# State tiles of four states by 32 channels in a decoder layer with a state-space block, in place of two by 64

## The chip, the cores and the metric

The kernel runs on one core of a Trainium2 chip. The time is the device time of one execution in microseconds (us); for the kernel before it is 5500.68 us, the median of three runs (5499.43 to 5505.06). Five engines take part: TensorE (PE) multiplies matrices and loads weights (PEld), VectorE (DVE) and ScalarE (ACT) work element by element, GpSimd (POOL) does a few small things and indirect transfers, and SyncE (SP) has the queue from which nearly all transfers (DMAs) are issued.

## What is computed

The reference is one decoder layer on x of 8 sequences x 512 tokens x 512 features, all in float32: a state-space (Mamba) block, cross-attention with 16 heads, and a mixture of 32 experts with a shared expert, each followed by a layer norm. The change is in the state-space block. Cut to that part (1024 channels d, 16 states n per channel):

```python
dA  = jnp.exp(A[None, None] * dt[..., None])                     # A = -exp(A_log), [d, n]
dBx = dt[..., None] * B_ssm[:, :, None, :] * x_main[..., None]

def scan_fn(h, inp):
    dA_t, dBx_t, C_t = inp
    h = dA_t * h + dBx_t                                         # [batch, d, n]
    y_t = jnp.einsum('bdn,bn->bd', h, C_t)                       # sum over the 16 states
    return (h, y_t)

y = ys + x_main * D_param
y = y * jax.nn.silu(z)
out = res_scale * (y @ out_proj_w) + residual
```

So each of the 16384 pairs (channel, state) has its own recurrence over 512 tokens; B and C depend on the state and the token but not on the channel, dt and x on the channel and the token but not on the state.

## The kernel before

**Tiles and steps.** Tokens go through the state-space block in chunks of T = 256, two to a sequence, 16 in all. Within a chunk, channels come in pairs of 128-channel tiles (index q, four pairs; i or ci says which of the two), and states in four groups (g). A step treats 128 channels x 4 states x 256 tokens, so a chunk has 32 steps and the kernel 512. The 128 partitions of a step's tile hold 64 channels twice, once for each half of the four states; along a row lie four blocks of 256 tokens, for two halves of channels (j) by two states (m).

A step does this:

- `decays` (L473): four exponentials on ACT, 128x256 each, write dA into one of two tiles `da`; dt comes from `both` (below).
- `carry` (L479): ACT copies the last state of the previous chunk into the first column of each block of a new tile `h` (four buffers).
- `steps_in` (L486): DVE multiplies dt*x by B into `h` (128x1024).
- `scan` (L493): DVE runs the recurrence along the whole row, 128x1028.
- `keep` (L498): ACT saves the last column for the next chunk.
- `collect` (L503): DVE multiplies `h` by C in place; then `products` has PE sum over the states. A product with the constant `twice` (128x64, two identity matrices of 64 one above the other) adds the two halves of the partitions; four such products of 256 columns add into `py` in PSUM, 64 partitions each. At g = 0 a product with the identity brings in D*x first.
- `gated` (L536), once per pair of channel tiles: DVE multiplies `py` by silu(z).

**Copies to other partitions.** B and C are computed for a chunk by `x_proj` and spilled to DRAM (`scr`). `bcast` (L411) reads two states of each back into every partition of a half, once for each q and g: four DMAs of 128 KB, six buffers. dt and dt*x are computed for a pair of channel tiles by `prepare` (L424) at step 3 of eight; its part `both` copies them into tiles whose halves of the partitions hold the same channels: eight DMAs of 128 KB, two buffers each.

**What lies beside the steps.** Between the DVE operations of the steps (`run(0)`, `run(1)`, `run(2)`) stand the other parts of the layer: projections for this chunk and the next (`convolve`, `gate_x`), the output product of the last chunk (`back`), and, in small pieces taken from a list by weight, the cross-attention, router and shared expert of the previous sequence (`units`). Of these the trace's views name: the convolution's taps (L376, `xs`), the softplus for dt (L445, L449, `dtx`), silu of z (L393), `dense`, the products of 512 columns at full width of the projections (L755), and in the attention the copies of a head's query and key rows (L804 to L808, `l_qa`, `l_ka`), the products for the scores (L818, L844), their maximum over keys on DVE (L820, `mx`), its copy into the query's rows (L834, `nm`) and the weighted sum of values (L860). `products` of a step are called in the next step, behind that step's scan. The framework then orders the instructions on each engine by its own estimate of when each is ready, so an engine's order isn't exactly that of the program. Each engine and SP's queue work strictly in the order they were given. After the 512 steps come the attention of the last sequence and the experts; the change doesn't touch them.

## Time and profile before

| | |
|---|---|
| median of three runs | 5500.68 us |
| the profiled execution: its time | 5514.39 us |
| its span, first to last instruction | 5512.7 us |
| PE busy | 4898.5 us (89%) |
| DVE busy | 4267.8 us (77%) |
| ACT busy | 2566.4 us (47%) |
| DMA packets | 769.84 MB, mean 140 GB/s |
| mean granted TensorE clock | 0.939 |
| steps of the state-space block | 64 to 3655 us |
| B and C to all partitions (L418) | 1024 DMAs of 128 KB |
| dt and dt*x to both halves (L458) | 512 DMAs of 128 KB |
| sums over states (L526) | 4096 records (two a product), 638.0 us busy |

A line of the groups reads: source line, engine, operation, written tile <- read tiles, shape, count | busy time in us, mean ns of one | idle time of the engine just before them, and what ended most of it. A line of waits reads: engine, tile and line that waited <- what ended the wait: us in total, times, longest. PEclk is the share of its full clock that TensorE was granted. Busy time is an average over stages with different limits, so stretches of the span are read one by one.

### The profile page before, as it was taken

To read this page: it belongs to the slowest core of one execution; us is meant where nothing else is said; L and a number is where in the kernel's file an instruction comes from. 1 tells how busy PE (TensorE), PEld (TensorE's weight loads), DVE (VectorE), ACT (ScalarE), POOL (GpSimd) and SP (SyncE) were. 2 spreads that over 40 slices of the span, in tenths; PEclk is the share of its full clock that TensorE was granted. 3 is DMA by queue.
4 is the path that set the end of the run, shared out by engine and by line. 5 is a ranking of instruction groups with operands and counts; after the bars stand their busy time and mean duration, and the time that the engine had idled before them with its cause. 6 is when DMAs were issued, how large, how long until landed. Compare 5 with 4: busy or idle time off the path is not lost. (4 is left out here: it accounts for less than half of the span.)

```text
span 5512.7 us, 60257 instructions
## 1 busy us (share of the span) xinstructions
PE 4898.5 (89%) x19752; PEld 2733.6 (50%) x19752; DVE 4267.8 (77%) x5370; ACT 2566.4 (47%) x5696; POOL 508.9 (9%) x424
## 2 busy tenths in 40 slices
PE   6668889899988988988998898889899999999994
PEld 3334344334434434443443443333577777777773
DVE  7898989889889898998989989953455665655554
ACT  5455555565556555556555655523222222222223
POOL 1000001001000100100100010010111111111111
PEclk8778999999999999999999999989999999999997
DMA  6887356345534635634553463441344454445454
GB/s 183 236 236 210 105 145 187 110 120 176 149 108 115 214 85 140 189 114 115 167 161 105 116 209 91 128 149 37 122 120 121 118 127 126 124 122 126 115 123 145
DMA packets 554283, 769.84 MB, mean 140 GB/s; under 512 B 135810, under 2 KB 268450, under 8 KB 551921
## 3 DMA queue, kind: packets, MB, share of 16 engines
q1 hardware_dynamic: 517952, 677.55, 42.0%
q0 software_dynamic: 33280, 76.90, 7.4%
q10 hardware_dynamic: 2736, 11.54, 0.5%
q8 instruction: 157, 2.57, 0.2%
q14 instruction: 158, 1.29, 0.1%
HBM read 508.68 MB, written 165.05 MB: 122 GB/s over the span
## 5 line engine op out<-in xcount | busy, mean ns | idle before, releaser
L496 DVE TENSOR_TENSOR_SCAN h<-l_da,h 128x1028 f32<-128x1028 f32 x512 | 1170.2, 2292 | 23.6 <-ACT h L483 5.6
L477 ACT ACTIVATE l_da<-both,l_aneg 128x256 f32<-128x256 f32 x2048 | 890.7, 499 | 362.4 <-DVE h L496 324.5
L526 PE MATMUL py<-h,l_twice 128*64 128x256 f32 x4096 | 638.0, 417 | 159.3 <-DVE h L506 111.7
L489 DVE TENSOR_TENSOR h<-both,bc 128x1024 f32<-128x1024 f32 x512 | 619.3, 1215 | 149.9 <-PE py L526 74.4
L506 DVE TENSOR_TENSOR h<-h,bc 128x1024 f32<-128x1024 f32 x512 | 621.2, 1218 | 6.1
L526 PEld LDWEIGHTS py<-h,l_twice 128*64 128x64 f32 x4096 | 304.5, 146 | 493.7 <-issue 232.8
L818 PE MATMUL ps_s<-l_ka,l_qa 64*128 64x512 f32 x1024 | 345.3, 698 | 155.0 <-DVE mx L820 153.8
L1307 PE MATMUL ps_h<-xT,w 128*128 128x320 f32 x1536 | 435.8, 433 | 0.0
L1387 POOL DMA_INDIRECT based<-y,xe x160 | 251.9, 1575 | 1316.4 <-ACT y L1410 571.9
L820 DVE TENSOR_REDUCE mx<-ps_s 128x2 f32<-128x1024 f32 x256 | 310.5, 1216 | 77.7 <-PE ps_s L818 76.5
L1328 DVE TENSOR_TENSOR hT<-ps_h,p 128x320 f32<-128x320 f32 x128 | 62.9, 492 | 379.2 <-PE ps_h L1307 379.2
L1307 PEld LDWEIGHTS ps_h<-xT,w 128*128 128x128 f32 x1536 | 292.5, 191 | 118.3 <-issue 0.5
L860 PE MATMUL po<-eT,l_va 128*64 128x512 f32 x1024 | 292.9, 647 | 11.2 <-ACT eT L848 7.5
L844 PE MATMUL ps_t<-l_qa,l_ka 64*128 64x512 f32 x1024 | 292.7, 642 | 8.6 <-ACT eT L848 8.5
L848 ACT ACTIVATE eT<-ps_t 128x1024 f32<-128x1024 f32 x256 | 259.2, 1013 | 67.4 <-PE ps_t L844 67.1
L501 ACT COPY l_state<-h 128x4 f32<-128x4 f32 x256 | 49.9, 195 | 511.6 <-DVE h L496 511.5
L1307 PE MATMUL ps_h<-t,s 128*128 128x320 f32 x1024 | 286.1, 432 | 0.0
L342 PE MATMUL ps_x<-xnT,wm 128*128 128x256 f32 x1024 | 252.8, 403 | 1.2 <-ACT xnT L331 1.0
L818 PEld LDWEIGHTS ps_s<-l_ka,l_qa 64*128 64x128 f32 x1024 | 94.3, 199 | 314.8 <-DVE mx L820 241.8
L342 PE MATMUL ps_z<-xnT,wm 128*128 128x256 f32 x1024 | 246.3, 395 | 4.3 <-DVE o L566 2.7
L755 PE MATMUL ps_p<-x2T,wa 128*128 128x512 f32 x512 | 247.8, 635 | 0.9 <-DVE hT L947 0.7
L693 POOL DMA_INDIRECT xbuf<-x2t,dest x128 | 183.4, 1433 | 625.1 <-DVE dest L684 281.8
(229 smaller groups left out, 7603.3 us busy)
## 6 DMA issues: line engine op xcount, KB each, us to landing
bc<-scr SPq DMA_DIRECT2D x1024, 128.0 KB
w<-in_w SPq DMA_DIRECT2D x93, 1024.0 KB
wm<-in_in_proj_w SPq DMA_DIRECT2D x128, 512.0 KB
xbuf<-zero SPq DMA_DIRECT2D x32, 1362.5 KB
xe<-xbuf SPq DMA_DIRECT2D x32, 1362.5 KB
both<-dt SPq DMA_DIRECT2D x256, 128.0 KB
both<-dtx SPq DMA_DIRECT2D x256, 128.0 KB
wm<-in_out_proj_w SPq DMA_DIRECT2D x64, 512.0 KB
```

Source lines behind the costliest of these rows:

```text
L342: nc.tensor.matmul(ps[:, i, :], w[:, dc, i * P : (i + 1) * P], f["xnT"][:, dc, :], start=(dc == 0), stop=(dc == DC - 1),)
L477: nc.scalar.activation(da[:, n, 1:], dt[:, c % 2, j, :], AF.Exp, scale=aneg[:, c, j, g, m : m + 1])
L489: nc.vector.tensor_tensor(steps, dtx[:, c % 2].unsqueeze(2).to_broadcast([P, 2, NG // 2, T]), bc[0], ALU.mult)
L496: nc.vector.tensor_tensor_scan(flat, da.rearrange("p n t -> p (n t)"), flat, 0.0, ALU.mult, ALU.add)
L506: nc.vector.tensor_tensor(steps[:, :, :, 0:T], steps[:, :, :, 1:], bc[1], ALU.mult)
L526: nc.tensor.matmul(py[j * HP : (j + 1) * HP, c % 2, :], twice, h[:, j * 2 + m, 0:T], start=False, stop=(s == (NST // NG - 1, NG // 2 - 1, 1)),
L818: nc.tensor.matmul(ps[:, j, :], qa[r, lt * P : (lt + 1) * P], ka[r, :], start=True, stop=True)
L820: return lambda: nc.vector.tensor_reduce(mx[:, lt, :].unsqueeze(2), ps, AX.X, ALU.max) and None
L844: nc.tensor.matmul(ps[:, j, :], ka[r, kc * P : (kc + 1) * P], qa[r, :], start=True, stop=True)
L848: nc.scalar.activation(eT, ps, AF.Exp)
L860: nc.tensor.matmul(po[j * 2 * HD : (j + 1) * 2 * HD, :], va[:, kc, i, j * HD : (j + 2) * HD], eT[:, j, :], start=(kc == 0), stop=(kc == SC ...
L1307: nc.tensor.matmul(ps, w[:, n, r * P : (r + 1) * P], x[:, n, :], start=not more and n == 0, stop=n == 1, skip_group_check=more,)
```

## The change

A step's tile now holds four quarters of the partitions: 32 channels, once for each of four groups of four states (`NQ = 4`, `QP = 32`). Along a row lie four blocks of 256 tokens, for two of the four groups of 32 channels (j) by the two channel tiles of the pair (i). A step is now (q, g, jj): state g of each group of four, and half jj of the channels of both tiles. There are still 32 steps in a chunk, of the same size.

- Two steps (jj = 0, 1) are summed together: `collect` keeps the first tile in `f["half"]`, and `products` of the second issues four products with `fold` (128x32, four identity matrices of 32) of 512 columns each, into 32 partitions of `py` each. The identity product is one of 128 partitions x 512 columns.
- B and C of a chunk are fetched once (`bcast`, for one g: eight DMAs of 32 KB) and kept for all four q, in eight buffers.
- dt and dt*x are copied by `repeat` into one tile for each of dt/dt*x and jj, one buffer each, in eight DMAs of 64 KB. The copy for the next pair is called for dt*x right after the last `steps_in` that reads the old one, for dt after the exponentials of steps 6 and 7 of eight.

```diff
@@ -27,8 +27,10 @@
 NT_ = T // P
-NG = 4
-HP = P // 2
+NG = NST // 4
+NQ = 4
+QP = P // NQ
+NB = 4
 NPB = 3
@@ -111,7 +113,7 @@
     mp = ctx.enter_context(tc.tile_pool(name="l_mamba", bufs=1))
-    bcp = ctx.enter_context(tc.tile_pool(name="l_bc", bufs=6))
+    bcp = ctx.enter_context(tc.tile_pool(name="l_bc", bufs=2 * NST // NG))
     cp = ctx.enter_context(tc.tile_pool(name="l_const", bufs=1))
@@ -127,8 +129,10 @@
 
-    twice = cp.tile([P, HP], F32, name="l_twice")
-    nc.vector.tensor_tensor(twice, ident[:, 0:HP], ident[:, HP:P], ALU.add)
+    fold = cp.tile([P, QP], F32, name="l_fold")
+    nc.vector.tensor_tensor(fold, ident[:, 0:QP], ident[:, QP : 2 * QP], ALU.add)
+    for r in range(2, NQ):
+        nc.vector.tensor_tensor(fold, fold, ident[:, r * QP : (r + 1) * QP], ALU.add)
 
@@ -187,14 +191,14 @@
 
-    aneg = cp.tile([P, CC, 2, NST // NG, NG // 2], F32, name="l_aneg")
+    aneg = cp.tile([P, CC, NQ, NG], F32, name="l_aneg")
 
 
     conv_tail = cp.tile([P, CC, 3], F32, name="l_conv_tail")
-    state = cp.tile([P, CC, NST // NG, NG], F32, name="l_state")
-    nothing = cp.tile([P, NG, 1], F32, name="l_nothing")
+    state = cp.tile([P, CC // 2, NG, 2, NB], F32, name="l_state")
+    nothing = cp.tile([P, NB, 1], F32, name="l_nothing")
     nc.gpsimd.memset(nothing, 0.0)
-    das = [mp.tile([P, NG, T + 1], F32, name=f"l_da{i}") for i in range(2)]
+    das = [mp.tile([P, NB, T + 1], F32, name=f"l_da{i}") for i in range(2)]
     for da in das:
...
@@ -411,15 +413,24 @@
         got = []
-        for r0 in (g * NG, NST + g * NG):
-            t = bcp.tile([P, NG // 2, T], F32, tag="bc", name="bc")
-            for r in range(2):
-                n0 = r0 + r * NG // 2
+        for r0 in (g, NST + g):
+            t = bcp.tile([P, T], F32, tag="bc", name="bc")
+            for s in range(NQ):
                 nc.sync.dma_start(
-                    t[r * HP : (r + 1) * HP], f["scr"][n0 : n0 + NG // 2, :].partition_broadcast(HP)
+                    t[s * QP : (s + 1) * QP], f["scr"][r0 + s * NG, :].partition_broadcast(QP)
                 )
-            got.append(t.unsqueeze(1).to_broadcast([P, 2, NG // 2, T]))
-        return got
+            got.append(t.unsqueeze(1).to_broadcast([P, NB, T]))
+        f["bc", g] = got
+
+    def repeat(f, q, what, jj):
+
+        to = mp.tile([P, 2, 2, T], F32, tag=f"rep{what}{jj}", name="rep")
+        src = f["ready", q][what]
+        for s in range(NQ):
+            for j in range(2):
+                r0 = (2 * jj + j) * QP
+                nc.sync.dma_start(to[s * QP : (s + 1) * QP, j], src[r0 : r0 + QP])
+        f["rep", what, q, jj] = to
 
@@ -450,13 +461,7 @@
                 nc.vector.tensor_tensor(dtx, dt, f["xs"][q], ALU.mult)
-                f["ready", q] = []
-                for src in (dt, dtx):
-                    to = mp.tile([P, 2, 2, T], F32, tag=f"both{len(f['ready', q])}", name="both", bufs=2)
-                    for r in range(2):
-                        for j in range(2):
-                            nc.sync.dma_start(to[r * HP : (r + 1) * HP, :, j, :], src[j * HP : (j + 1) * HP])
-                    f["ready", q].append(to)
+                f["ready", q] = dt, dtx
                 return wait(timesD)
@@ -470,66 +475,59 @@
 
-    def decays(c, g, dt, da):
-
-        for n in range(NG):
-            j, m = n // 2, n % 2
-            nc.scalar.activation(da[:, n, 1:], dt[:, c % 2, j, :], AF.Exp, scale=aneg[:, c, j, g, m : m + 1])
-
-    def carry(t, c, g):
-
-        last = state[:, c, g].unsqueeze(2)
-        h = mp.tile([P, NG, T + 1], F32, tag="h", name="h", bufs=4)
+    def decays(f, q, g, jj, da):
+
+        dt = f["rep", 0, q, jj]
+        for n in range(NB):
+            j, i = n // 2, n % 2
+            nc.scalar.activation(
+                da[:, n, 1:], dt[:, j, i, :], AF.Exp, scale=aneg[:, 2 * q + i, 2 * jj + j, g : g + 1]
+            )
+
+    def carry(t, q, g, jj):
+
+        last = state[:, q, g, jj].unsqueeze(2)
+        h = mp.tile([P, NB, T + 1], F32, tag="h", name="h", bufs=4)
         nc.scalar.copy(h[:, :, 0:1], last if t else nothing)
         return h
 
-    def steps_in(c, h, dtx, bc):
-
-        steps = h.rearrange("p (j m) t -> p j m t", j=2)[:, :, :, 1:]
+    def steps_in(f, q, g, jj, h):
+
+        dtx = f.pop(("rep", 1, q, jj)) if g == NG - 1 else f["rep", 1, q, jj]
         nc.vector.tensor_tensor(
-            steps, dtx[:, c % 2].unsqueeze(2).to_broadcast([P, 2, NG // 2, T]), bc[0], ALU.mult
+            h[:, :, 1:], dtx.rearrange("p j i t -> p (j i) t"), f["bc", g][0], ALU.mult
         )
 
-    def scan(t, c, g, da, h):
+    def scan(da, h):
 
         flat = h.rearrange("p n t -> p (n t)")
         nc.vector.tensor_tensor_scan(flat, da.rearrange("p n t -> p (n t)"), flat, 0.0, ALU.mult, ALU.add)
 
-    def keep(t, c, g, h):
+    def keep(t, q, g, jj, h):
 
         if t < S // T - 1:
-            nc.scalar.copy(state[:, c, g].unsqueeze(2), h[:, :, T : T + 1])
-
-    def collect(c, g, h, bc, f):
-
-        steps = h.rearrange("p (j m) t -> p j m t", j=2)
-        nc.vector.tensor_tensor(steps[:, :, :, 0:T], steps[:, :, :, 1:], bc[1], ALU.mult)
-        xs = f["xs"][c // 2]
+            nc.scalar.copy(state[:, q, g, jj].unsqueeze(2), h[:, :, T : T + 1])
+
+    def collect(f, q, g, jj, h):
+
+        nc.vector.tensor_tensor(h[:, :, 0:T], h[:, :, 1:], f["bc", g][1], ALU.mult)
+        if jj == 0:
+            f["half"] = h
+            return
+        hs, xs = (f.pop("half"), h), f["xs"][q]
 
         def products():
-            if g == 0 and c % 2 == 0:
+            if g == 0:
                 f["py"] = psy.tile([P, 2, T], F32, tag="py", name="py")
-            py = f["py"]
-
-            if g == 0:
-                for j in range(2):
-                    nc.tensor.matmul(
-                        py[j * HP : (j + 1) * HP, c % 2, :],
-                        ident[:, j * HP : (j + 1) * HP],
-                        xs[:, c % 2, :],
-                        start=(c % 2 == 0),
-                        stop=False,
-                    )
-            for m in range(NG // 2):
-                for j in range(2):
-                    s = (g, m, c % 2)
-                    nc.tensor.matmul(
-                        py[j * HP : (j + 1) * HP, c % 2, :],
-                        twice,
-                        h[:, j * 2 + m, 0:T],
-                        start=False,
-                        stop=(s == (NST // NG - 1, NG // 2 - 1, 1)),
-                    )
+                nc.tensor.matmul(f["py"], ident, xs, start=True, stop=False)
+            for j in range(NQ):
+                nc.tensor.matmul(
+                    f["py"][j * QP : (j + 1) * QP, :, :],
+                    fold,
+                    hs[j // 2][:, 2 * (j % 2) : 2 * (j % 2) + 2, 0:T],
+                    start=False,
+                    stop=g == NG - 1,
+                )
 
@@ -1054,7 +1052,7 @@
     chunks = [(b, t) for b in range(B) for t in range(S // T)]
-    steps = [(q, g, i) for q in range(CC // 2) for g in range(NST // NG) for i in range(2)]
+    steps = [(q, g, jj) for q in range(CC // 2) for g in range(NG) for jj in range(2)]
     def do(fn, *args, first=False):
@@ -1088,11 +1086,16 @@
     dry()
-    bc, n = bcast(f, 0), 0
+    n = 0
+    for g in range(NG):
+        bcast(f, g)
+    for what in range(2):
+        for jj in range(2):
+            repeat(f, 0, what, jj)
     nc.scalar.activation(aneg, aneg, AF.Exp)
     nc.vector.tensor_scalar(aneg, aneg, -1.0, None, ALU.mult)
-    decays(0, 0, f["ready", 0][0], das[0])
-    ahead, products = carry(0, 0, 0), None
+    decays(f, 0, 0, 0, das[0])
+    ahead, products = carry(0, 0, 0, 0), None
     old, side, cleared = None, [], 0
@@ -1104,12 +1107,12 @@
             whole = sum(own) + sum(x[0] for x in side)
-        for k, (q, g, ci) in enumerate(steps):
-            if ci == 0:
-                if (q, g) != (CC // 2 - 1, NST // NG - 1):
-                    bcn = bcast(f, (g + 1) % (NST // NG))
-                else:
-                    bcn = bcast(nf, 0) if after else None
+        for k, (q, g, jj) in enumerate(steps):
+            if i and k == 1:
+                bcast(f, NG - 1)
+            if after and 28 <= k < 31:
+                bcast(nf, k - 28)
+            qf, nq = (f, q + 1) if q + 1 < CC // 2 else (nf, 0)
             h = ahead
@@ -1159,7 +1162,9 @@
 
-            steps_in(2 * q + ci, h, f["ready", q][1], bc)
+            steps_in(f, q, g, jj, h)
+            if g == NG - 1 and (qf is f or after):
+                repeat(qf, nq, 1, jj)
             if k % 8 == 1:
@@ -1174,22 +1179,22 @@
             run(0)
-            scan(t, 2 * q + ci, g, das[n % 2], h)
+            scan(das[n % 2], h)
             n += 1
 
             if k + 1 < len(steps) or after:
-                nq, ng, ni = steps[(k + 1) % len(steps)]
-                ahead = carry(t if k + 1 < len(steps) else after[1], 2 * nq + ni, ng)
-                decays(2 * nq + ni, ng, (f if k + 1 < len(steps) else nf)["ready", nq][0], das[n % 2])
-            keep(t, 2 * q + ci, g, h)
+                then = steps[(k + 1) % len(steps)]
+                ahead = carry(t if k + 1 < len(steps) else after[1], *then)
+                decays(f if k + 1 < len(steps) else nf, *then, das[n % 2])
+                if k % 8 in (5, 6) and (qf is f or after):
+                    repeat(qf, nq, 0, k % 8 - 5)
+            keep(t, q, g, jj, h)
             run(1)
 
             if products:
                 products()
-            products = collect(2 * q + ci, g, h, bc, f)
+            products = collect(f, q, g, jj, h)
             run(2)
-            if ci == 1:
-                bc = bcn
             while i < 2 and cleared < E * (i * len(steps) + k - 6) // (2 * len(steps) - 7):
```

## The prediction

> **What bounds the kernel now.** I read the stages first: busy time of each engine in stretches of the span. The state updates run from 64 to 3655 us, two chunks to a stretch of about 456 us; then come the last batch's attention (to 4090) and the experts.
>
> ```profile
> core 0: us, PE busy (x) PEld busy (x) DVE busy (x) ACT busy (x) POOL busy (x), PEclk, DMA share, GB/s
> 64.00:518.00 454.00, 311.37 (x1247) 167.84 (x1244) 404.50 (x380) 241.18 (x597) 14.91 (x12) 0.79 0.80 229
> 518.00:974.00 456.00, 407.32 (x1676) 194.27 (x1678) 416.93 (x455) 264.19 (x594) 31.84 (x29) 0.96 0.52 147
> 1430.00:1886.00 456.00, 407.28 (x1669) 193.41 (x1670) 410.64 (x450) 262.27 (x589) 32.17 (x29) 0.95 0.49 141
> 4090.00:5513.00 1423.00, 1350.93 (x5525) 997.77 (x5523) 818.93 (x1534) 401.86 (x867) 227.76 (x145) 0.98 0.49 124
> ```
>
> VectorE (DVE) and TensorE (PE) are each busy about 90% in the middle stretches. The first stretch has no attention beside it: PE is busy 69% there, and yet the stretch is as long, with DVE at 89%. So DVE is the bound and PE the near second. Summed over the eight stretches to 3655, DVE is busy 3226.7 of 3591 us and idle 364; a change that leaves DVE's work alone can only move those 364 us. Next, what DVE waited for between 64 and 3655 us (total us, times, longest):
>
> ```profile
> DVE h L489 <- PE py L526: 74.4, 55, 3.4
> DVE dtx L449 <- ACT dtx L445: 38.5, 18, 8.8
> DVE h L489 <- DMA both<-dtx: 35.6, 12, 6.3
> DVE mx L820 <- PE ps_s L818: 31.1, 28, 2.3
> DVE zs L540 <- ACT zs L393: 27.6, 8, 4.1
> DVE xs L376 <- ACT xs L368: 26.2, 25, 2.5
> DVE zs L540 <- PE py L526: 19.6, 14, 4.2
> DVE h L489 <- DMA bc<-scr: 15.4, 7, 4.6
> DVE h L489 <- DMA l_qa<-qT: 15.4, 5, 3.7
> ```
>
> With the small rows below them PE ends 142 us of it, ScalarE (ACT) about 92 in three rows, DMAs about 66. Then the groups, for durations:
>
> ```profile
> L496 DVE TENSOR_TENSOR_SCAN h<-l_da,h 128x1028 f32<-128x1028 f32 x512 | 1170.2, 2292 | 23.6 <-ACT h L483 5.6
> L526 PE MATMUL py<-h,l_twice 128*64 128x256 f32 x4096 | 638.0, 417 | 159.3 <-DVE h L506 111.7
> L489 DVE TENSOR_TENSOR h<-both,bc 128x1024 f32<-128x1024 f32 x512 | 619.3, 1215 | 149.9 <-PE py L526 74.4
> ```
>
> A step is L489 + L496 + L506 = 1.22 + 2.29 + 1.22 = 4.73 us of DVE; 512 steps are 2420 us. Each product appears as two instructions (2048 products, 4096 records). Last, the timeline near 2010 and 2030 us, for the pitch of products and of DMA issues:
>
> ```profile
> 2007.95 1.08 PE L860 MATMUL po<-eT,l_va 128*64 128x512 f32 x4
> 2009.29 1.04 PE L526 MATMUL py<-h,l_twice 128*64 128x256 f32 x8
> 2025.93 2.71 SPq L458 DMA_DIRECT2D both<-dt  x4
> 2028.74 2.55 SPq L458 DMA_DIRECT2D both<-dtx  x4
> 2031.39 0.57 SPq L804 DMA_DIRECT2D l_qa<-qT  x1
> ```
>
> **The change, part by part.** *DVE and ACT: nothing.* A tile is still 128 x 4 x 256: 512 scans, 1024 multiplies, 2048 exponentials, 512 carries of unchanged size. Two more additions of 128x32 at the start lie beside the first loads. The state's product with the identity becomes one of 512 full-width columns in place of four half-width ones of 256: 0.97 us (L755: 247.8 us for 256 products) against two rounds of about 0.48, equal.
>
> *PE: the sums.* Before, 2048 products of 256 columns, 64 wide, the two halves side by side: four take 1.04 us with their tail, about 0.95 from one group to the next, so 0.48 a round of two. After, 1024 products of 512 columns, 32 wide, four of which can lie side by side. They don't always stand together: in the order of the built instructions they come in 317 runs, 121 of exactly four, but 166 shorter, because a tile's two products go out when its own multiply is done. Rounds: a run of n takes n/4 rounded up, 351 in all; before, n/2 rounded up gives 1069. If a round of four costs what L860's round of 512 columns costs (0.95 pitch), that is 351 x 0.95 = 333 us against 1069 x 0.48 = 513: 180 us less, 5.8% of PE's 3112 us. The trace shows two side by side, not four. From above, no gain beyond two: a run of four takes two rounds, and 1024/2 x 0.95 = 486, 27 us less. From below, 333. The Trainium skill (TensorE: Matmul & The Clock Gate, Part 3, measured speedup) gives 2.38 times for three column tiles of 32; at the same 79% four give 3.2, an estimate of 4 x 0.97/3.2 = 1.21 us a round, 425 us, 88 less. The trace's own pair overlaps fully (0.48 a round against 2 x 0.48 for two full-width products of 256), so I take 180. The halved weight loads are hidden (PEld is idle most of the time).
>
> What is it worth? DVE waited for PE in the three PE rows above 97 times, 125 us, 1.3 us a time. Such waits end stretches in which PE is full: 24 to 36 us at 1850 to 1874 or 1610 to 1646, in windows of 12 us. 5.8% of 24 to 36 us is 1.4 to 2.1 us, as much as a wait; but the densest bursts (projections, output products) hold fewer sums than the mean. I take two thirds of 142: -95. Of the 92 us that ACT ended, part is ACT held up itself (the copy of the carry waits 250 us for L526): a fifth, -18. Together -113.
>
> The rule that speaks against it: the same page, Part 1, says that idle gaps of a few us halve PE's clock. The trace agrees: granted 0.79 in the first stretch with PE 69% busy, 0.95 with 90%, and 0.59 in 1478 to 1490. PE would go to about 84% busy; on the line between those rows that is 0.91 instead of 0.95, and 4.5% slower over 385 us a stretch gives back 17 of its 22 us. By that rule the sum is near -25 instead of -113. But most windows in which PE is full show 1.00: the slow clock falls where PE has slack, so I keep -113 and let the rule widen the range.
>
> *SP's queue.* Removed: 1024 issues for B and C become 512 (32 KB instead of 128). Added: dt and dt*x go out in four bursts of 8 issues for each pair of channel tiles, 2048 in place of 512. In all 1024 more. L458 shows 8 issues in 5.4 us; the like of the new ones (32 rows x 512 elements) is L804, 0.57, pitch 0.61. So 8 take 4.9 us and the last lands about 1.8 us later (L458's last issue at 2028.0, ACT goes on at 2029.9): 6.7 us. SP's whole burst per pair is 32 x 0.61 = 20 us of the 56 that a pair lasts; before 8 x 0.67 = 5.4. Bytes: B and C 134 to 17 MB, dt and dt*x 67 to 134.
>
> What hides it: the new copy has one buffer per half (two before), so its DMA waits for the last multiply that reads the old one, and the first multiply of the next pair waits for it. In the built DVE order I added durations between these two: first half 9.7 us at least, median 12.4, against 6.7; second half, from the same start, 19.1 at least, median 25.7, against 24 to 32 issues: 16.4 to 21.3 us. Each pairing taken for itself, none is late. The scheduler makes room: it often puts the multiply of the next state group of the first half ahead of the second half's. So the burst costs nothing on DVE while SP is free when a buffer is released. If that cover goes, a late multiply holds DVE's whole queue: the scan behind it, the collecting multiply, then PE's sums. And behind the burst itself stand weights, the query and key rows and the maxima (L804 to L808, L834), which can be 15 us later than now. Bounds: from below, the B and C wait (15) vanishes and nothing comes; from above, 2 us at each of 127 halves, +250. Nearest row: before, with 8 issues and two buffers, DVE waited 35.6 us for dt*x in 12 of 64 cases, and 15.4 for qT. I take these doubled, less the 15: +36, and +15 for attention rows that hold up PE: about +50.
>
> **Sum.** -113 + 50 = -63 on the profiled execution, 5514.4 (span 5512.7 and 1.7 around it), so 5451; the median of the runs is 13.7 lower, **5440** (rounded up from 5437).
>
> **Rivals.** *Nothing to be had* (5500): DVE is the bound and the clock eats PE's gain. For: the first stretch, as long with a light PE. Against: that stretch's idle had other enders (its DMA share is 0.80). *The coupling breaks* (5300): all 142 us of PE, 50 of ACT's 92 and the 15 go, -200. Against: dense bursts stay. *SP's bursts decide* (5560): if SP stands blocked or behind other work so that a half is 3 us late in 58 of 127 cases, +170 against -113. It decides from about 1.8 us of lateness at every pair. For: in the trace SP waits often for a buffer (L418 for L506, 395 us), and the margin is 3 us in the thinnest first halves. Against: L418's blocking issues are halved and released early. *The change doesn't do what it says* (products never four abreast): relief 27 of 180, then -17 + 50, 5530; it is counted with the slower case.
>
> **How the numbers follow.** Chances: the forecast 0.43 (own range 5380 to 5488), coupling breaks 0.15, nothing 0.12, slower cases 0.30. About 0.2% (11 us) is what a measurement can tell from no change. Of "nothing" 0.09 lies within it, 0.02 below, 0.01 above: faster 0.60, same 0.09, slower 0.31. Range 5330 to 5570: it cuts half of "coupling breaks" and the far end of the slower case.
>
> **What would show it.** Sums: about 2048 records, 380 us busy or less instead of 638, eight of them in about 1.05 us. DVE's wait for py under 40 us, for bc about zero. DVE's wait for the copy of dt*x under 80 us in all; over 150 the SP rival is right. The granted clock in the middle stretches 0.91 to 0.95. DVE busy unchanged at 3227, and a stretch 448 us instead of 456. I am wrong if a run of four takes twice the time of a pair, or if DVE's idle moves to ACT or DMA rows one for one.

## The result: 5.9% slower

The changed kernel takes 5828.39 us (median of four runs, 5813.34 to 5832.82) against 5502.87 in the same comparison: 1.0586 times as long, interval 1.0564 to 1.0607. The forecast was 5440, and the upper end of the range 5570. The profiled execution took 5829.17 us, its span 5827.5.

Nearly all of it is in the state-space part. That now runs from 83 to 3979 us, 3896 us long instead of 3591; the first 83 us, before it, were 64. What follows takes 1848 us (1858 before). Stretches of the span, two chunks each, and last the experts:

```profile
core 0: us, PE busy (x) PEld busy (x) DVE busy (x) ACT busy (x) POOL busy (x), PEclk, DMA share, GB/s
83.00:558.00 475.00, 272.78 (x808) 117.56 (x807) 385.48 (x354) 223.90 (x554) 13.79 (x12) 0.72 0.62 191
558.00:1050.00 492.00, 393.11 (x1330) 162.75 (x1330) 408.91 (x451) 259.40 (x578) 38.00 (x29) 0.88 0.42 119
1542.00:2034.00 492.00, 404.41 (x1366) 169.02 (x1365) 408.24 (x447) 261.78 (x584) 31.81 (x29) 0.89 0.42 119
4402.00:5827.00 1425.00, 1355.75 (x5547) 1001.89 (x5545) 824.44 (x1542) 403.49 (x870) 232.59 (x145) 0.98 0.47 125
```

A middle stretch is 492 us instead of 456. VectorE (DVE) is busy 408 us in it, as before; the added 36 us are idle. Over all stretches to 3979, DVE is busy 3217 us (3227 before) and idle 679 (364 before). So its work did not grow; it waits 315 us more. TensorE (PE) is no longer full either: 82% of a stretch, at a granted clock of 0.89. Which waits grew, from the waits of DVE and then of PE between 83 and 3979 us (total us, times, longest):

```profile
DVE mx L818 <- PE ps_s L816: 144.7, 50, 10.0
DVE h L497 <- PE py L524: 117.0, 62, 6.1
DVE h L497 <- DMA rep<-dtx: 101.0, 13, 13.2
DVE h L504 <- ACT l_da L483: 58.2, 31, 6.3
DVE o L564 <- PE po L555: 36.6, 8, 7.5
```

```profile
PE py L524 <- DVE h L513: 450.2, 101, 21.5
```

Before, DVE waited 74.4 us for py, 31.1 for ps_s and 35.6 for the copies of dt*x, and PE waited 111.7 us for h. Now DVE waits for PE's scores and sums, and PE waits 450 us for DVE's tiles: each waits for the other, and of DVE's waits only some 100 us are ended directly by a copy. No row names a single culprit; the experiments had to find it. The groups for the sums and the multiply that waits:

```profile
L524 PE MATMUL py<-h,l_fold 128*32 128x512 f32 x2048 | 462.5, 692 | 510.5 <-DVE h L513 450.2
L497 DVE TENSOR_TENSOR h<-rep,bc 128x1024 f32<-128x1024 f32 x512 | 613.1, 1215 | 277.4 <-DMA rep<-dtx 126.2
```

What a late copy looks like where one is seen, in the timeline (start, duration, engine; SPq is the SyncE (SP) queue's issuing):

```profile
1537.23 1.19 DVE L497 TENSOR_TENSOR h<-rep,bc 128x1024 f32<-128x1024 f32 x1
1543.08 0.68 DVE L462 TENSOR_TENSOR dt<-dt,l 128x512 f32<-128x512 f32 x1
1543.83 0.51 SPq L432 DMA_DIRECT2D rep<-dt  x1
1545.06 0.34 SPq L725 DMA_DIRECT2D vd<-v  x1
1545.45 2.42 SPq L432 DMA_DIRECT2D rep<-dt  x4
1545.96 0.67 DVE L463 TENSOR_TENSOR dtx<-dt,xs 128x512 f32<-128x512 f32 x1
1549.25 0.35 SPq L725 DMA_DIRECT2D vd<-v  x1
1549.65 1.78 SPq L432 DMA_DIRECT2D rep<-dt  x3
1551.84 4.95 SPq L432 DMA_DIRECT2D rep<-dtx  x8
1559.17 1.22 DVE L497 TENSOR_TENSOR h<-rep,bc 128x1024 f32<-128x1024 f32 x1 [11.27 <-DMA rep<-dtx]
```

dt is made at 1543.8 and dt*x at 1546.6. SP issues the eight copies of dt, between them two stores (L725) that wait for ACT, and comes to dt*x only at 1551.8. DVE stands still for 11.3 us. Both halves' buffers had been free since 1538.4, when the last multiply that read the old copies ended: what is late is the queue. Waits of this length are rare: eight of DVE's multiplies in this part of the trace, about one in two chunks, wait 10 us or more.

### The profile page after: what moved, and what is told of

Read it like the earlier page. It is cut to its first block, busy times and chain, and to the rows that moved or that the text cites. A ratio compares the mean times of both kernels' runs of the same rounds, so it can differ in the third digit from the quotient of the medians.

```text
span 5827.5 us, 56423 instructions
## 1 busy us (share of the span) xinstructions
PE 4844.7 (83%) x17320; PEld 2526.6 (43%) x17320; DVE 4256.2 (73%) x5372; ACT 2571.1 (44%) x5688; POOL 524.8 (9%) x424
## 5 line engine op out<-in xcount | busy, mean ns | idle before, releaser
L483 ACT ACTIVATE l_da<-rep,l_aneg 128x256 f32<-128x256 f32 x2048 | 886.2, 498 | 364.7 <-DVE h L504 342.6
L524 PE MATMUL py<-h,l_fold 128*32 128x512 f32 x2048 | 462.5, 692 | 510.5 <-DVE h L513 450.2
L497 DVE TENSOR_TENSOR h<-rep,bc 128x1024 f32<-128x1024 f32 x512 | 613.1, 1215 | 277.4 <-DMA rep<-dtx 126.2
L816 PE MATMUL ps_s<-l_ka,l_qa 64*128 64x512 f32 x1024 | 371.4, 731 | 59.9 <-DVE mx L818 58.8
L524 PEld LDWEIGHTS py<-h,l_fold 128*32 128x32 f32 x2048 | 62.3, 114 | 783.3 <-DVE h L513 388.2
L842 PE MATMUL ps_t<-l_qa,l_ka 64*128 64x512 f32 x1024 | 332.6, 669 | 46.1 <-DVE mx L818 17.8
L858 PE MATMUL po<-eT,l_va 128*64 128x512 f32 x1024 | 307.2, 657 | 13.3 <-ACT eT L846 13.3
L691 POOL DMA_INDIRECT xbuf<-x2t,dest x128 | 212.7, 1662 | 676.5 <-DVE dest L682 610.3
L555 PE MATMUL po<-wm,zs 128*128 128x512 f32 x512 | 250.1, 635 | 13.8 <-ACT nm L829 9.7
```

The lines of the kernel that those rows point to most:

```text
L483: nc.scalar.activation(da[:, n, 1:], dt[:, j, i, :], AF.Exp, scale=aneg[:, 2 * q + i, 2 * jj + j, g : g + 1])
L497: nc.vector.tensor_tensor(h[:, :, 1:], dtx.rearrange("p j i t -> p (j i) t"), f["bc", g][0], ALU.mult)
L524: nc.tensor.matmul(f["py"][j * QP : (j + 1) * QP, :, :], fold, hs[j // 2][:, 2 * (j % 2) : 2 * (j % 2) + 2, 0:T], start=False, stop=g == N ...
L816: nc.tensor.matmul(ps[:, j, :], qa[r, lt * P : (lt + 1) * P], ka[r, :], start=True, stop=True)
L842: nc.tensor.matmul(ps[:, j, :], ka[r, kc * P : (kc + 1) * P], qa[r, :], start=True, stop=True)
L858: nc.tensor.matmul(po[j * 2 * HD : (j + 1) * 2 * HD, :], va[:, kc, i, j * HD : (j + 2) * HD], eT[:, j, :], start=(kc == 0), stop=(kc == SC ...
```

## The experiments

Of each change to the code only the lines that matter are shown; a line of dots marks a gap.

### Is it the copies?

**The changed kernel without the copies** but the first pair's, which all pairs read:

```diff
-        dt = f["rep", 0, q, jj]
+        dt = once["rep", 0, 0, jj]
...
-        dtx = f.pop(("rep", 1, q, jj)) if g == NG - 1 else f["rep", 1, q, jj]
+        dtx = once["rep", 1, 0, jj]
...
-            if g == NG - 1 and (qf is f or after):
-                repeat(qf, nq, 1, jj)
...
-                if k % 8 in (5, 6) and (qf is f or after):
-                    repeat(qf, nq, 0, k % 8 - 5)
```

> The changed kernel, but every step reads the copies of dt and dt*x made for the first pair of channel tiles: the other 2016 copy DMAs are left out (so the state updates work on wrong dt). Theory COPIES (32 DMA issues a pair on one queue, made shortly before their first use, hold DVE and what stands behind it): the 101 us that DVE waits for dt*x, the 58 us for the decays and most of the extra waits for PE vanish, 5430 to 5520. Theory ORDER (sums of a pair of steps stand at the head of PE's queue and wait for DVE while attention stands behind them): at most the 101 + 58 us go, 5670 or more.

5432.94 us, 0.9863 of before (0.9824 to 0.9902). The copies cost 395 us; all the rest of the change together brings 70, or 77 against the 5509.63 us that the kernel before took beside this run. In this kernel's profile:

```profile
L526 PE MATMUL py<-h,l_fold 128*32 128x512 f32 x2048 | 423.3, 641 | 150.6 <-DVE h L515 98.8
508.00:946.00 438.00, 377.35 (x1331) 161.83 (x1330) 396.06 (x439) 252.16 (x566) 38.41 (x28) 0.93 0.30 90
DVE h L499 <- PE py L526: 160.3, 72, 7.0
```

A stretch is 438 us, the clock 0.93, and PE's wait ahead of the sums is back to 151 us from 510. So the 450 us of PE waiting for DVE are a consequence of the copies, not of the sums' new form.

### Is it the single buffers, or the place of the calls?

**First half double-buffered and copied as soon as dt*x is made:**

```diff
-        to = mp.tile([P, 2, 2, T], F32, tag=f"rep{what}{jj}", name="rep")
+        to = mp.tile([P, 2, 2, T], F32, tag=f"rep{what}{jj}", name="rep", bufs=2 - jj)
...
                 f["ready", q] = dt, dtx
+                for what in range(2):
+                    repeat(f, q, what, 0)
...
-            if g == NG - 1 and (qf is f or after):
+            if g == NG - 1 and jj and (qf is f or after):
...
-                if k % 8 in (5, 6) and (qf is f or after):
-                    repeat(qf, nq, 0, k % 8 - 5)
+                if k % 8 == 6 and (qf is f or after):
+                    repeat(qf, nq, 0, 1)
```

> The changed kernel with two buffers for the copies of dt and dt*x of the first half of the channels, copied as soon as they are made, as the kernel before did; the second half stays single and late. COPIES, if it is the buffer and the late place that count: half or more of the loss goes, 5600 to 5680. COPIES, if it is the number of issues after dt is made: little moves, 5780 to 5840, since dt*x is still made just before its use and 16 issues still come first. ORDER: 5780 to 5840.

5828.22 us: no change at all. Neither the release of the first half's buffer nor the place of its call sets the time.

**Six tiles `h` instead of four:**

```diff
-        h = mp.tile([P, NB, T + 1], F32, tag="h", name="h", bufs=4)
+        h = mp.tile([P, NB, T + 1], F32, tag="h", name="h", bufs=6)
```

> The changed kernel with six state tiles in place of four. If the first tile of two being held a step longer is what costs (a third theory, BUFFERS): the 117 us that DVE waits for the sums go and with them waits of ACT, 5650 to 5720. COPIES: the state tiles aren't short, 5790 to 5830. ORDER: 5760 to 5830.

5860.13 us, above all that was expected. More state tiles don't help.

**The sums kept in the program's order on PE:**

```diff
-                nc.tensor.matmul(
+                tc.keep_in_program_order(nc.tensor.matmul(
                     f["py"][j * QP : (j + 1) * QP, :, :],
...
```

> The changed kernel with the sums' products kept in program order on PE, so that the four of two steps stand together far more often (203 runs of four in place of 121) and the first tile's two no longer go ahead of the second's. ORDER: moves the time by 50 us or more, likely down, to 5700 to 5780. COPIES: within 30 us of 5828.

5767.87 us, 60 less than with the planned order, as the theory of the order had it. The same work in another order is worth tens of us, so differences of that size between other kernels here say little. It leaves most of the loss.

### Is it the use of the copies, or the issuing?

**All copies issued, none read.** Every pair reads the first pair's; the later copies go to one buffer for dt and one for dt*x:

```diff
-        to = mp.tile([P, 2, 2, T], F32, tag=f"rep{what}{jj}", name="rep")
+        to = mp.tile([P, 2, 2, T], F32, tag=f"{tag}{what}{jj if tag == 'once' else 0}", name="rep")
...
-        dt = f["rep", 0, q, jj]
+        dt = once["rep", 0, 0, jj]
...
-        dtx = f.pop(("rep", 1, q, jj)) if g == NG - 1 else f["rep", 1, q, jj]
+        dtx = once["rep", 1, 0, jj]
```

> The changed kernel with all 2048 copy DMAs issued in their places, but nobody reads them: the steps read the first pair's copies (so the state updates work on wrong dt). What is left of COPIES is then only what the issues do to the other work behind them in SP's queue. QUEUE (the issues delay weights, query and key rows and maxima): 5700 to 5830. LATE (DVE and ACT wait for the copies themselves): 5430 to 5500.

5835.03 us, as long as with the copies read. Nobody waits for a copy, and the time is lost all the same. (With one buffer a copy also waits for the one before it into that buffer.) By the waits of its trace from 83 to 3980 us, transfers end only 43 us of DVE's idle, 32 of PE's and 23 of ACT's. The rest of the loss is engines waiting for one another:

```profile
DVE h L499 <- PE py L526: 377.8, 74, 19.8
PE py L526 <- DVE h L515: 259.2, 69, 18.2
```

**The kernel before with its copies cut in four** (16 rows each, the same bytes):

```diff
-                            nc.sync.dma_start(to[r * HP : (r + 1) * HP, :, j, :], src[j * HP : (j + 1) * HP])
+                            for s in range(4):
+                                w0, s0 = r * HP + s * HP // 4, j * HP + s * HP // 4
+                                nc.sync.dma_start(to[w0 : w0 + HP // 4, :, j, :], src[s0 : s0 + HP // 4])
```

> The kernel before with its 8 copy DMAs a pair of channel tiles split into 32 of 16 partitions each, at their place and with two buffers. If the number of issues alone is the cause: 5700 or more. If it takes the late place or the single buffer as well: 5510 to 5580.

6052.82 us, 1.1004 of before (1.0982 to 1.1026). Nothing of the change is in this kernel, only 1536 more issues on SP's queue: 0.36 us of kernel time for each. Its page has much the same picture as the changed kernel's, with more waiting at the copies themselves:

```profile
L491 DVE TENSOR_TENSOR h<-both,bc 128x1024 f32<-128x1024 f32 x512 | 611.8, 1213 | 366.4 <-DMA both<-dtx 174.9
both<-dtx SPq DMA_DIRECT2D x1024, 32.0 KB
```

**The kernel without copies, with 32 unrelated transfers a pair:** a constant is copied to a spare tile, and nothing else reads or writes that tile.

```diff
+    def idle():
+        for s in range(NQ):
+            for j in range(2):
+                nc.sync.dma_start(spare[s * QP : (s + 1) * QP, j], w_dt[:, j * 2 * T : (j + 1) * 2 * T])
...
+            if g == NG - 1 and (qf is f or after):
+                idle()
...
+                if k % 8 in (5, 6) and (qf is f or after):
+                    idle()
```

> The kernel without copies (nocopy, 5433 us: the state updates work on wrong dt) with 32 DMAs a pair of channel tiles put back in the copies' places that copy a constant of the same size (32 rows x 512) into a spare tile: they wait for nothing that is computed and nobody waits for them. OCCUPANCY (SP's time for the issues alone delays what stands behind): 5700 to 5850. BLOCKING (what costs is that the first copy waits at the head of SP's queue for dt or for a buffer, with the other transfers behind it): 5440 to 5560.

5689.02 us: 256 of the 395 us come back, with no dependence on anything that is computed. (A transfer still waits for an earlier one; SP spends 68 us on these waits in the whole trace.) **The same with 16:**

```diff
-            for j in range(2):
-                nc.sync.dma_start(spare[s * QP : (s + 1) * QP, j], w_dt[:, j * 2 * T : (j + 1) * 2 * T])
+            nc.sync.dma_start(spare[s * QP : (s + 1) * QP, 0], w_dt[:, 0 : 2 * T])
```

> The copies left out but the first pair's (dt of the first pair is used throughout), and 16 DMAs of a constant a pair in their places, where the earlier kernel had 32 (5689, against 5433 without). THRESHOLD: SyncE's queue has room for 16, so 5390 to 5460. LINEAR: half of the 256 us, about 5560.

5459.81 us: 27 us for the first 16, no more than another order can make, and 229 for the second. It isn't so much per issue; the queue has room for some of them.

### Another queue, fewer issues

**All copies from GpSimd's queue** (`nc.sync` becomes `nc.gpsimd` in `repeat`):

> The changed kernel with the copies issued from GpSimd's queue in place of SP's. QUEUE: SP's other transfers are free again, 5480 to 5600, unless GpSimd issues more slowly than SP. LATE: the copies themselves are no earlier, 5650 to 5830.

5686.78 us: better than on SP's queue, worse than without, and in the range for copies that are no earlier. GpSimd's queue then has the whole burst, and DVE waits for the copies directly:

```profile
DVE h L497 <- DMA rep<-dt: 152.8, 15, 24.2
```

**Half on each queue:**

```diff
-                nc.sync.dma_start(to[s * QP : (s + 1) * QP, j], src[r0 : r0 + QP])
+                (nc.sync, nc.gpsimd)[j].dma_start(to[s * QP : (s + 1) * QP, j], src[r0 : r0 + QP])
```

> The changed kernel with 16 of the 32 copies of a pair (the second group of channels of each half) issued from GpSimd's queue, the other 16 from SyncE's. All is computed. OCCUPANCY of SyncE's queue with a threshold: 16 issues a pair cost nothing there (5393 with 16 in all), and GpSimd adds some part of what all 32 on it cost (5687 against 5433), half or less: 5420 to 5560, about 5490. Number of DMAs or bytes, whichever queue: 5650 to 5830.

5476.70 us, 0.9959 of before (0.9945 to 0.9973), in the lower half of what was expected. All is computed, every byte of the copies is still moved, and 352 us are gone. Its waits:

```profile
PE py L524 <- DVE h L513: 148.0, 62, 12.9
DVE h L497 <- DMA rep<-dtx: 109.1, 24, 12.2
DVE h L497 <- PE py L524: 87.8, 39, 5.6
```

DVE still waits 109 us for copies of dt*x, as long as in the slow kernel. What shrank is PE's 450 us wait for DVE, to 148, and DVE's wait for the scores, from 144.7 to 8.8 us.

**The attention's row copies on GpSimd's queue,** the state copies left on SP's. In the functions that fetch query and key rows, maxima and results, lines like this one:

```diff
-                nc.sync.dma_start(qa[r1 : r1 + HD, :], st["qT"][r0 : r0 + HD, i // 2, :])
+                nc.gpsimd.dma_start(qa[r1 : r1 + HD, :], st["qT"][r0 : r0 + HD, i // 2, :])
```

> The changed kernel with the attention's row copies (queries, keys, maxima, results: 24 DMAs a pair of heads) issued from GpSimd's queue, so that they no longer stand behind the copies of dt. If these rows are what the copies hold up: 5550 to 5700. If it is other work (weights, or the copies themselves): 5780 to 5880.

5641.98 us, 186 less than the changed kernel. Not one of the added issues was touched: what stood beside them in the queue was taken out, and nearly half of the loss went with it.

**16 copies a pair,** where both channel groups of a half read the first group's rows (so dt and dt*x are wrong for the other; the two lines that read them are not shown):

```diff
-            for j in range(2):
-                r0 = (2 * jj + j) * QP
-                nc.sync.dma_start(to[s * QP : (s + 1) * QP, j], src[r0 : r0 + QP])
+            nc.sync.dma_start(to[s * QP : (s + 1) * QP, 0], src[2 * jj * QP : 2 * jj * QP + QP])
```

> The changed kernel with 16 copies a pair of channel tiles in place of 32: the second group of channels in a row isn't copied and reads the first group's rows (wrong dt for half of the channels). OCCUPANCY: the loss over nocopy halves, 5600 to 5660. BLOCKING: the waits at the head of the queue stay, 5720 to 5820.

5393.08 us, 0.9797 of before (0.9779 to 0.9815). Both expectations missed: 16 copies a pair cost nothing that could be seen.

**Through DRAM:** dt and dt*x are stored once, and one read for each channel group spreads it to all four quarters; 10 issues a pair (the two stores are not shown).

```diff
-        for s in range(NQ):
-            for j in range(2):
-                r0 = (2 * jj + j) * QP
-                nc.sync.dma_start(to[s * QP : (s + 1) * QP, j], src[r0 : r0 + QP])
+        for j in range(2):
+            r0 = (2 * jj + j) * QP
+            nc.sync.dma_start(
+                to[:, j].rearrange("p i t -> p (i t)"), src[r0 : r0 + QP, :].unsqueeze(0).to_broadcast([NQ, QP, 2 * T])
+            )
```

> The changed kernel with dt and dt*x written to DRAM once (2 DMAs a pair of channel tiles) and read back by 8 DMAs of 128 partitions, 10 issues in place of 32, the buffers and places of the reads unchanged. If the number of issues is the cause (QUEUE or LATE): 5430 to 5560. If it is the single buffer or the place: 5780 or more, since the way over DRAM takes longer.

6244.91 us, the slowest of all; the number of issues alone does not decide. The store has to land before the reads can start, and DVE waits for them at nearly every half:

```profile
DVE h L502 <- DMA rep<-dtd: 690.1, 105, 20.7
```

Few issues don't help when each comes late by itself.

**dt and dt*x in one tile, copied together:** 16 issues a pair of 128 KB, first half double-buffered, all computed.

```diff
-        to = mp.tile([P, 2, 2, T], F32, tag=f"rep{what}{jj}", name="rep")
+        to = mp.tile([P, 2, 2, 2, T], F32, tag=f"rep{jj}", name="rep", bufs=2 - jj)
...
-                nc.sync.dma_start(to[s * QP : (s + 1) * QP, j], src[r0 : r0 + QP])
+                nc.sync.dma_start(to[s * QP : (s + 1) * QP, :, j], src[r0 : r0 + QP])
```

> The changed kernel with dt and dt*x of a pair in one tile, so that one DMA of 32 rows x 1024 elements copies both: 16 issues a pair instead of 32, of 128 KB instead of 64, all on SyncE's queue; the first half has two buffers and is copied as soon as dt*x is made. All is computed, the bytes are unchanged. OCCUPANCY with a threshold: 16 issues cost nothing, 5380 to 5470, about 5420, provided that an issue of 128 KB takes about 0.65 us as before (L458: 0.68). BYTES or the length of the copies: above 5550.

5826.13 us: the expectation missed. An issue takes 0.65 us as assumed, so SP issues as little as in the fast kernels with 16, and yet the time is that of 32. At one place in its timeline:

```profile
1532.89 0.67 DVE L465 TENSOR_TENSOR dt<-dt,xs 128x512 f32<-128x512 f32 x1
1533.58 5.09 SPq L432 DMA_DIRECT2D rep<-dt  x8
1542.86 1.22 DVE L500 TENSOR_TENSOR h<-rep,bc 128x1024 f32<-128x1024 f32 x1 [8.03 <-DMA x1d<-o]
```

The copies are issued the moment dt*x is made (1533.6), the last at about 1538, and DVE goes on 4 us after that, having waited 8 us (the row names the transfer whose event came last). But such places are few: before the multiplies that wait on a copy, from 83 us on, DVE is idle 77 us in all, against 135 in the changed kernel and 172 in the one with half on each queue, added up over the trace. The loss looks like the changed kernel's again:

```profile
L527 PE MATMUL py<-h,l_fold 128*32 128x512 f32 x2048 | 477.0, 728 | 490.6 <-DVE h L516 431.1
```

### Late on the chip, or a worse order?

The framework orders each engine's instructions by its own estimate, so every kernel above differs from the others in its order too. **Two kernels with the order fixed:** all instructions of PE, DVE and ACT in these layers stay in the order of the program, and are in the same order in both (in the two traces DVE's and ACT's follow one another identically to the end of this part); one has the copies, the other is the kernel without them.

```diff
+            r = got(*args, **kw)
+            if r is not None:
+                self.tc.keep_in_program_order(r)
...
+        self.vector, self.tensor = Kept(tc, tc.nc.vector), Kept(tc, tc.nc.tensor)
+        self.scalar = Kept(tc, tc.nc.scalar)
...
-    nc = tc.nc
+    nc = KeptNC(tc)
```

> The changed kernel with all instructions of TensorE, VectorE and ScalarE in the state-space and attention part in the order in which the program calls them, not in the order that the framework plans; SyncE's queue is planned as before. It is to be read only against its twin, the same kernel with every copy but the first pair's left out (wrong dt): these three engines have the same order in both. LATE TRANSFERS (the issues hold transfers up on the chip, and engines wait for them): this kernel is 250 to 450 us slower than its twin, with DVE rows ended by DMAs. PLAN (the framework, which sees the transfers late, writes a worse order): less than 100 us between the two, since the order can't be changed. The level is unknown, since the program's own order hides less: 5600 to 6300.

> The twin: the same fixed order of the three engines, and every copy but the first pair's left out (dt and dt*x of the first pair are used throughout, so the result is wrong). LATE TRANSFERS: 250 to 450 us faster than the kernel with the copies. PLAN: within 100 us of it, and slower than 5433, which the planned order gave without the copies.

5938.67 us with copies and 5567.12 without: 372 us between them. So the copies cost about as much when the order cannot change: transfers that are late on the chip are enough for the loss. Here they show directly (waits of DVE and of ACT in the kernel with copies; all lines are L100 because one helper records them):

```profile
DVE mx L100 <- PE ps_s L100: 180.7, 64, 6.1
DVE h L100 <- DMA rep<-dtx: 151.2, 51, 6.8
ACT l_da L100 <- DMA rep<-dt: 173.6, 43, 12.1
```

In the twin without copies the two DMA rows are gone, but for 27.8 and 19.8 us at the start (65 to 82 us), for the first pair; the wait for the scores is

```profile
DVE mx L100 <- PE ps_s L100: 52.6, 34, 3.4
```

In the planned orders, by contrast, the direct waits are small and the mutual ones large.

### The other terms of the sum

**The kernel before with B and C fetched once per chunk,** the second part of the change alone:

```diff
-    bcp = ctx.enter_context(tc.tile_pool(name="l_bc", bufs=6))
+    bcp = ctx.enter_context(tc.tile_pool(name="l_bc", bufs=2 * NST // NG))
...
-            if ci == 0:
-                if (q, g) != (CC // 2 - 1, NST // NG - 1):
-                    bcn = bcast(f, (g + 1) % (NST // NG))
-                else:
-                    bcn = bcast(nf, 0) if after else None
+            if i and k == 1:
+                bcast(f, NST // NG - 1)
+            if after and 28 <= k < 31:
+                bcast(nf, k - 28)
+            bc = f["bc", g]
```

> The kernel before with one part of the change alone: B and C fetched once per chunk (16 DMAs a chunk in place of 64; its tile layout, copies and sums stay). OCCUPANCY: 768 issues fewer at 0.35 us each and DVE's waits for bc gone, but DVE stays the bound: 5380 to 5460. BLOCKING: 5470 to 5505.

5415.90 us, 0.9841 of before (0.9828 to 0.9855): faster than both kernels, with everything computed. It has 768 issues fewer on SP's queue.

```profile
DVE h L489 <- PE py L526: 52.7, 38, 3.4
L526 PE MATMUL py<-h,l_twice 128*64 128x256 f32 x4096 | 622.1, 411 | 128.4 <-DVE h L506 78.5
```

The wait for bc had been 15 us in the profile before; the gain is 87. The waits for py (74.4) and PE's own wait for h (111.7) shrank as well, though nothing of the sums was touched. The framework's order changes with the edit too, so part of the 87 may be the order.

**The kernel before with half of its sums** (states of odd m only, so the result is wrong):

```diff
-            for m in range(NG // 2):
+            for m in range(NG // 2 - 1, NG // 2):
```

> The kernel before with every second product of the sums left out (states of odd m do not enter the result, so it is wrong): 1024 products of 256 columns fewer, about 535 rounds of 0.48 us, 257 us of TensorE. It measures by itself what less work for TensorE in the sums is worth there. STEP (b) as forecast (113 of 180 us come back): about -160, 5340. If TensorE's work is hardly on the path (the kernel without copies, with 176 us less of sums, was no faster than the kernel before with only B and C fetched once): 5460 to 5510.

5401.52 us, 0.9814 of before (0.9799 to 0.9829), between the two theories.

```profile
L526 PE MATMUL py<-h,l_twice 128*64 128x256 f32 x2048 | 395.1, 434 | 218.3 <-DVE h L506 134.8
```

243 us less of PE (638.0 to 395.1) bring 101: 0.42 us for each, again with another order.

### Side by side

SP's issuing is the time in which its queue was busy issuing between the first scan and the last, added up over the trace, with its share of that stretch.

| kernel | copies a pair on SP's queue | SP issuing, us | time, us |
|---|---|---|---|
| before, B and C once | 8 | 1190 (34%) | 5416 |
| changed, no copies | 0 | 917 (26%) | 5433 |
| no copies, 16 unrelated | 16 | 1530 (43%) | 5460 |
| changed, 16 copies | 16 | 1534 (44%) | 5393 |
| changed, half on each queue | 16 (16 on GpSimd's) | 1570 (44%) | 5477 |
| before | 8 | 1643 (46%) | 5503 |
| changed, dt and dt*x in one copy | 16 of 128 KB | 1622 (41%) | 5826 |
| changed, attention rows on GpSimd's | 32 | 1744 (47%) | 5642 |
| no copies, 32 unrelated | 32 | 2171 (58%) | 5689 |
| changed | 32 | 2171 (56%) | 5828 |
| changed, all on GpSimd's queue | 0 (32 on GpSimd's) | 957 (25%) | 5687 |
| changed, through DRAM | 10 | 1818 (42%) | 6245 |
| before, copies cut in four | 32 | 2564 (62%) | 6053 |

Where the copies lie on SP's queue as single transfers, the times roughly follow the third column: at 26 to 44% of issuing they lie between 5393 and 5477 us, at 47 to 62% between 5642 and 6053. That is no threshold. The loss itself lengthens the stretch of which the share is taken; the kernel before stands at 46% with 5503, and with half of its sums at 47% with 5402. All on GpSimd's queue and the way through DRAM lose by direct waits for their copies instead. One copy for both is the exception that the column doesn't explain: the issuing isn't all.

**What the traces add.** Two more things can be read from them. The first is the chain of work, followed back from the last scan to the first, at each step to what released an instruction or to the one before it on its engine. SP's queue holds 511 of the chain's 3897 us in the changed kernel, 74 of 3583 in the kernel before, 17 of 3495 without the copies, and 734 against 32 in the pair with the fixed order. So the queue does lie on the path, though few waits end at a copy. The second is the order: how many places an instruction of PE stands, on average, from its place in another kernel's trace, up to the last scan.

| kernel | SP's queue in the chain, us | places from the changed kernel | places from the one with 16 copies | time, us |
|---|---|---|---|---|
| changed, 16 copies | 180 | 8.1 | 0 | 5393 |
| changed, dt and dt*x in one copy | 211 | 2.2 | 8.5 | 5826 |
| changed, attention rows on GpSimd's | 362 | 7.1 | 1.9 | 5642 |
| changed | 511 | 0 | 8.1 | 5828 |

The kernel with one copy for both has nearly the slow kernel's order, and little of SP's queue in its chain; the one with the rows moved has nearly a fast kernel's order, and much of the queue. Both are slow. This answers the exception as far as reading can: the order that the framework writes, and transfers that are late on the chip, each seem enough for a loss of 200 us and more. The kernels with unread and with 32 unrelated transfers stand 12.8 and 14.4 places from the one without copies, so their loss need not be lateness alone either.

**What stays open.** How the 395 us divide between late transfers and the order. The fixed pair shows that lateness is enough; for the order there is only the reading above. To run the order planned for the changed kernel without the copies, or a slow kernel's work in a fast kernel's order, would tell; it wasn't tried.

## Why the prediction was wrong

**"SP's queue" is the step that failed.** It was put at +50, bounds -15 to +250; the copies cost +395. The burst itself was right: 2016 issues of 0.61 us, 20 us a pair. Three things in the reasoning were not:

- The cover was counted from the release of the old buffer to the first use of the new one. Double-buffering the first half moved nothing, so there that margin was not what counts. When dt and dt*x are made and where SP then stands came on top: in the timeline above the buffer is free, and SP is still at dt's copies when dt*x is due.
- "Behind the burst stand weights, rows and maxima, up to 15 us later" was priced at 15 us. With the rows moved to another queue, 186 us went. The step priced the waits at the copies, doubled from the row before, and not what a 20 us burst does to a queue that already issued 46% of the time. The upper bound, 2 us at each of 127 halves, had the same fault.
- No term stood for the order that the framework writes when SP's queue is fuller. By the reading above it carries a part of the loss; how large a part stays open.

The rival "SP's bursts decide" came nearest, with 5560 instead of 5828, though it too priced late halves at DVE. Its sign, a wait for dt*x of over 150 us, did not appear (101.0): the loss shows as DVE and PE waiting for each other.

**"PE: the sums": mechanism right, size too large.** Four products lie side by side, almost without loss:

```profile
1562.75 1.07 PE L524 MATMUL py<-h,l_fold 128*32 128x512 f32 x8
1572.11 1.04 PE L524 MATMUL py<-h,l_fold 128*32 128x512 f32 x2
```

Eight records, four products, take 1.07 us; one product alone takes 1.04. Over the trace it is the same: at full clock the median is 1.07 us for 96 runs of four and 1.05 for 31 single ones. So the lower bound, no gain beyond two, and the factor from the Trainium skill's page (TensorE: Matmul & The Clock Gate, Part 3), which would make a round 1.21 us, are both too dear here. The sums' busy time fell by 176 us (638.0 to 462.5), as worked out (180), though it stayed above the 380 announced. The broken runs were counted: 361 in the trace, against 351 rounds in the prediction, and at 1.05 to 1.07 us they would make some 384. What was left out is the slow clock: a run took 1.28 us on average. Without copies the sums take 423 us, and 367 in the fixed order without copies, where 221 of 291 runs hold four products. But what 180 us of PE are worth was put at 113; by the halved sums (0.42) it is about 75, an estimate.

**B and C were undersized.** -15, the visible wait; alone they bring -87. The sum without the copies would then be near -160, and -70 was measured (interval some 20 us each way). A likely place of the missing 90 is a row: without copies DVE waits 160.3 us for py where it waited 74.4 before, 86 more. Two steps' tiles are now summed together, so the first of them is held until the second is done, with four tiles in all. That was only argued; six tiles were tried only with the copies in place, where they brought nothing.

**The clock.** 0.91 to 0.95 was announced; it is 0.89 with PE busy 82%, and 0.93 without copies at 86%. The line that the prediction drew between two stretches gives 0.89 at 82% and 0.92 at 86%, so it held; the reason for setting it aside, that the slow clock falls where PE has slack, does not hold throughout (in the kernel before, PE is busy for all of 1490 to 1502 us at a clock of 0.69). The rule of the same page, that gaps of a few us lower the clock, agrees with the direction. But PE is idle because it waits for DVE, so the slow clock follows the loss here; no run separates what it adds.

**"DVE and ACT: nothing"** held: 3217 us against 3227. The expected stretch of 448 us was 438 without the copies.

## What to carry to other kernels

A queue that issues transfers in order is a resource like an engine: add up its issues times their duration for each stage, and beside it everything else that goes through the same queue. Where that sum nears half of the stage, as here, the price of further issues isn't read from the wait at their own consumers. A change that makes compute cheaper by copying more, in smaller pieces, should be costed in issues first; half of them on another queue was worth more here than anything done about buffers. And where a framework plans the order, compare the orders of two kernels before their times: an edit to one queue can move every engine's work.

## What the hardware showed that was not expected

- The issue on SP's queue takes about 0.61 us for an on-chip copy of 32 rows of 2 KB and 0.65 for 32 rows of 4 KB: between these two the bytes hardly matter. Cutting copies in four at equal bytes cost 0.36 us of kernel time for each added issue in the kernel before.
- On GpSimd's queue the same 64 KB copy takes 0.50 us to issue, and lands 2.6 to 3.1 us after it (medians for dt and dt*x, with half and with all of the copies there).
- A read from DRAM that spreads 32 rows to four quarters of the partitions takes 1.2 us to issue (504 of them 603 us), twice a copy within the on-chip memory.
- Four float32 products of 512 columns, each 32 wide, overlap almost fully: 1.07 us against 1.04 for one.
